# One correction over 1354 columns, and the narrow factor on GpSimd, in a graph-attention loop

## The chip, the cores and the metric

The kernel runs on one core of one Trainium2 chip. A core has a matrix engine (TensorE, PE in the profile, with its weight loads as PEld), VectorE (DVE), ScalarE (ACT), GpSimd (POOL) and a queue engine that issues transfers (SyncE, SP). The engines run side by side, each through its own list of instructions in order, and wait for each other on semaphores. The metric is device time in microseconds of one execution. Half a percent of it is 5.3 us.

## The reference, cut to what matters

Four graph layers run one after the other on x (2708 nodes by 128 features) with the same adjacency matrix adj (2708 by 2708, float32), each followed by a residual sum and a normalization of the rows. The change lies in the second layer, the attention:

```python
XW = X @ W
s_col = XW @ a[0, :f];  s_row = XW @ a[0, f:]
Z1  = leaky_relu(s_row[:, None] + s_col[None, :], negative_slope=0.01)
den = exp(Z1)
num = A @ den
att = where(num != 0, den / where(num != 0, num, 1.0), 0.0)
H   = A @ (att @ XW)
```

The quotient needs 1/num for a matrix of 2708 by 2708. The kernel finds it as exp(-log(num)) on ScalarE, improves it by one Newton step on VectorE, and multiplies it by the part of den that is a maximum of a row value and a column value.

## The kernel before

Earlier stages compute the first layer, the features XW in sorted order (`xws`), the row factors `gb` (a value for each node along the columns, the same on all partitions), the column factors `g_inv`, and the weights `lw` of a short form of A @ den: with the columns sorted, den of a block of columns can be built from the rows of adj that belong to that block and two carried rows of sums.

The layer then runs as a loop of 44 passes, `for i, (h, q) in enumerate(steps)`: two halves h of the output columns (1354 each, `HALF`), and 22 pairs q of blocks in each half. The instructions of the loop stand on every engine in the order in which they are written here, since the loop is under `tc.manual_schedule`. The 1354 columns of a pass are handled in two pieces: wide (1024 columns, `WIDE`) and narrow (330, `NARROW`), because the sums stay in PSUM, where the wide piece has two buffers and the narrow one has one.

One pass, by the names that the change and the prediction use:

- `load(i + 2)`: GpSimd issues two indirect gathers of 126 rows of adj into a strip of `ring` (L1306), and SP issues two small copies of the carried rows into the same strip (L1312). There are three strips, so the strip of pair i + 2 is free when the num of pair i - 1 has been computed. In the first eight passes `fetch_xw` adds one more gather on GpSimd (L895).
- `find_num(i, "narrow")` and `find_num(i + 1, "wide")`: TensorE multiplies the gathered rows by `lw` into `num` (L1428).
- `add(i - 1)`: TensorE multiplies the finished quotient `inv` of the pass before by `xws` and adds it to `hacc` (L1285).
- `find_inv(i, "narrow")`, `find_inv(i + 1, "wide")`: ScalarE computes log and exp (L1260, L1263). In the first half it also scales a tile of `xws` (L1475).
- `mix_1` (L1270): VectorE computes err = inv x num, for each piece. `keep` (L1443) has SP copy two rows of err to `carry`.
- `mix_2` (L1274), the correction: inv = (err - 2) x inv, for each piece.
- `mix_3` (L1277), the factor: inv = max(gb, g_inv) x inv, for each piece.

So TensorE's order is narrow num of pass i, wide num of pass i + 1, hacc of pass i - 1. GpSimd's order is the gathers of pair i + 2, then, in the first passes, the fetch of a tile of `xws`. One more GpSimd instruction, the power of 22 values for `dinv` (L257), belongs to a later layer and stands among the first passes.

Of the kernel before, what the change touches and what calls it, by code (L numbers as in the profile page):

```python
# [8 lines left out]
F32 = mybir.dt.float32  # L9
# [7 lines left out]
P = 128  # L17
# [3 lines left out]
BJ = 62  # L21
# [31 lines left out]
def kernel(  # L53
# [16 lines left out]
    nc = tc.nc  # L70
# [67 lines left out]
    ones = const.tile([P, 1], F32, tag="ones", name="ones")  # L138
    nc.vector.memset(ones, 1.0)

    def load_const(src, cols, name):
        t = const.tile([P, cols], F32, tag=name, name=name)
        nc.sync.dma_start(t, src)
        return t

    def load_rows(src, cols, name):

        return load_const(bass.AP(tensor=src.tensor, offset=src.offset, ap=[[0, P], [1, cols]]), cols, name)

    def row_tile(name):  # L150
        return big.tile([P, T * D], F32, tag="hT", name=name)
# [216 lines left out]
    with tc.tile_pool(name="knn", bufs=1) as knn:  # L368
# [97 lines left out]
        with (  # L466
# [5 lines left out]
            for c in range(C):  # L472
                w = cw[c]
                load_x(chunk_tiles[c])
                parts = [load_panel(g, c, load if g < G - 1 else None) for g in range(G)]
                nc.sync.dma_start(
                    res[:, : FULL - S, cols[c]],
                    adjT[S * P : FULL * P, cols[c]].rearrange("(t p) k -> p t k", p=P),
                )
                if LAST:  # L480
                    nc.sync.dma_start(res[few(c), FULL - S, cols[c]], adjT[FULL * P :, cols[c]])
                both = degp.tile([P, 2, CW], F32, tag="both", name="both")
                nc.vector.tensor_add(both[:, :, :w], parts[0][:, :2, :w], parts[0][:, 2:, :w])
                more = [part[:, n : n + 2, :w] for part in parts[1:] for n in (0, 2)]
                more += [res[:, n : n + 2, cols[c]] for n in range(0, RES, 2)]
                for m in more:
                    nc.vector.tensor_add(both[:, :, :w], both[:, :, :w], m)  # L487
                nc.vector.tensor_add(both[:, 0, :w], both[:, 0, :w], both[:, 1, :w])

                for g in range(min(c, G)):  # L490
                    add_group(c, g, parts[g])
                    if wait is not None:
                        add_group(*wait)
                        wait = None
                if c == C - 1:
# [12 lines left out]
                inv_sqrt(dinv[:, t0:t1], deg[:, t0:t1])  # L508
                scale_rows(y, xs, dinv, ts)
                if c == C - 1:  # L510
                    spread(y[:, FULL, :])
                wait = (c, c, parts[c] if c < G else None, c == C - 1)
                if c == C - 2:
                    w1_sb = load_const(w1, D, "w1")
                    w2_sb = load_const(w2, D, "w2")
                    wa_sb = load_const(w_att, D, "w_att")
                    wl_sb = load_const(w_lap_t, D, "w_lap")
                    wx_sb = load_const(w_cat_t[:D, :], D, "w_cat_x")
                    wh_sb = load_const(w_cat_t[D:, :], D, "w_cat_h")
                    b1_sb = load_rows(b1, D, "b1")  # L520
                    b2_sb = load_rows(b2, D, "b2")
                    bl_sb = load_rows(b_lap, D, "b_lap")
                    bc_sb = load_rows(b_cat, D, "b_cat")
                    a_sb = load_rows(a_att, 2 * D, "a_att")


            def rest(c, g, end=False):
# [726 lines left out]
    del slots[SLOTS:]  # L1254
    more.close()

    def invert(w, num, pool, bufs, sums=True):
        inv = pool.tile([P, w], F32, tag=f"inv{w}", name="inv", bufs=bufs)
        if sums:
            nc.scalar.activation(inv, num[:, :w], AF.Ln, scale=plain[:, 0:1], bias=plain[:, 1:2])  # L1260
        else:
            nc.scalar.activation(inv, num[:, :w], AF.Ln)
        nc.scalar.activation(inv, inv, AF.Exp, scale=-1.0)  # L1263
        return inv

    def mix_1(w, num, inv, pool):
        err = pool.tile([P, w], F32, tag=f"err{w}", name="err")
        nc.vector.tensor_mul(err, inv, num[:, :w])  # L1270
        return err

    def mix_2(inv, err):
        nc.vector.scalar_tensor_tensor(inv, err, 2.0, inv, op0=ALU.subtract, op1=ALU.mult)  # L1274
# [47 lines left out]
    def dense_layer():  # L1322
# [3 lines left out]
        with (  # L1326
# [68 lines left out]
            for h in range(2):  # L1395
                hacc = dps.tile([P, 3 * CW], F32, tag="hacc", name="hacc")
                for q in range(NQ):
# [10 lines left out]
                    inv = invert(HALF, num, dense, 1, sums=False)  # L1408
                    mix_2(inv, mix_1(HALF, num, inv, dense))
                    mix_3(HALF, q, inv, h * HALF)  # L1410
                    add_up(HALF, q, inv, hacc)
                nc.scalar.copy(mT[:, h * HALF : (h + 1) * HALF], hacc[:, :HALF])
    def block_layer():
        with (
# [7 lines left out]
            def find_num(i, piece):  # L1422
                q, (c0, w, bufs) = steps[i][1], pieces[piece]
                num = nums[i, piece] = ops.tile([P, w], F32, tag=f"num{w}", name="num", bufs=bufs)
                for o in range(0, w, CW):
                    e = min(w, o + CW)
                    for n in range(2):
# [2 lines left out]
                            rhs=rows[i][:, n, c0 + o : c0 + e], start=True, stop=True,  # L1430
                        )

            def find_inv(i, piece):
                invs[i, piece] = invert(pieces[piece][1], nums[i, piece], own, 3)

            def keep(i, piece, err):

                (h, q), (c0, w, _) = steps[i], pieces[piece]
                for n in range(2):
                    b = block(2 * q + n) + 1  # L1440
                    if b % CH:
                        o = h * HALF + c0
                        nc.sync.dma_start(  # L1443
                            carry[2 * b : 2 * b + 2, o : o + w], err[n * (BJ + 2) : n * (BJ + 2) + 2, :]
                        )

            def add(i):
# [1 line left out]
                if q == 0:  # L1449
                    haccs[h] = ops.tile([P, 3 * CW], F32, tag="hacc", name="hacc")  # L1450
                for piece, (c0, w, _) in pieces.items():
                    add_up(w, q, invs[i, piece], haccs[h][:, c0 : c0 + w])

            engines = {nc.tensor, nc.vector, nc.scalar, nc.sync, nc.gpsimd}
            with tc.manual_schedule(engines={e.engine for e in engines}):
# [5 lines left out]
                for i, (h, q) in enumerate(steps):  # L1461
# [13 lines left out]
                        nc.scalar.mul(xws[:, q, :], xws[:, q, :], g_col[:, q : q + 1])  # L1475
                    if (h, q) == (1, 0):
                        nc.scalar.copy(mT[:, :HALF], haccs[0][:, :HALF])
                    if i + 1 < len(steps):
                        errs = {}
                        for piece, (c0, w, _) in pieces.items():  # L1480
                            errs[piece] = mix_1(w, nums[i, piece], invs[i, piece], own)
                            keep(i, piece, errs[piece])
                        for piece in pieces:
                            mix_2(invs[i, piece], errs[piece])
                        for piece, (c0, w, _) in pieces.items():
                            mix_3(w, q, invs[i, piece], h * HALF + c0)
                    else:
                        for piece, (c0, w, _) in pieces.items():
                            mix_2(invs[i, piece], mix_1(w, nums[i, piece], invs[i, piece], own))
                            mix_3(w, q, invs[i, piece], h * HALF + c0)  # L1490

                for t0 in range(0, EARLY, WIDE // P):
                    ts = range(t0, min(t0 + WIDE // P, EARLY))
# [130 lines left out]
```

## Time and profile before

| what | us |
|---|---|
| median of 3 runs (1063.95 to 1068.74) | 1066.62 |
| the profiled execution | 1068.2 |
| its span, first to last instruction | 1066.5 |
| TensorE matmul busy in the span | 990.4 |
| VectorE busy | 643.2 |
| ScalarE busy | 339.1 |
| GpSimd busy | 265.6 |
| 88 gathers into ring, mean of one | 1.115 |
| err, 88 instructions of two shapes, mean | 0.853 |
| correction, 88 of two shapes, mean | 0.863 |
| factor, 88 of two shapes, mean | 0.913 |

The span is the time from the first to the last instruction of the program; the execution's own time is 1.7 us longer. Busy times are of one profiled execution. The end of a matmul is modelled in the profile, so where a pace is wanted it is read from the starts of instructions and not from busy time. The three means of VectorE mix a form of 1024 columns with one of 330; in the loop the two forms of err take 1209 and 497 ns, of the correction 1237 and 491, of the factor 1273 and 551 (520 to 700 us of the span).

### The profile page before, as it was taken

The numbers are of one execution on the slowest core, as the hardware profiler recorded it, in microseconds if no ns is written. First come the engines' busy times: TensorE is split into PE (matmuls) and PEld (weight loads), VectorE is DVE, ScalarE is ACT, GpSimd is POOL, SyncE is SP. The second block draws the span as 40 slices with busy tenths as digits, with TensorE's granted clock in tenths as the row PEclk, the third lists the DMA queues.
The fourth block names the chain that finished last, engine by engine and source line by source line (L and its number), as shares of the span: only waits on it lengthen the run. The fifth ranks groups of instructions, "written<-read, shape, count | busy, mean of one in ns | idle before, by whom it ended". The sixth has DMA issues, their size and how long they took to land.

```text
span 1066.5 us, 11423 instructions
## 1 busy us (share of the span) xinstructions
PE 990.4 (93%) x3678; PEld 479.8 (45%) x3678; DVE 643.2 (60%) x1351; ACT 339.1 (32%) x614; POOL 265.6 (25%) x332
## 2 busy tenths in 40 slices
PE   0898999999998999699899999999999999999996
PEld 0345554444434566444333333334444544564444
DVE  5985438999954678764789999995121111132222
ACT  0000125555510235603767777663010100010000
POOL 4000000000447664107774444440121100000000
PEclk9989999999999999699999999999999999999998
DMA  9999350000056756399655546456765856575652
GB/s 338 367 342 249 115 166 1 0 1 1 22 199 211 239 175 207 126 341 306 165 160 131 147 135 164 137 151 208 226 198 173 291 196 202 159 256 170 225 173 67
DMA packets 109363, 190.30 MB, mean 178 GB/s; under 512 B 13650, under 2 KB 46690, under 8 KB 109294
## 3 DMA queue, kind: packets, MB, share of 16 engines
q1 hardware_dynamic: 91582, 151.86, 43.8%
q0 software_dynamic: 17712, 37.62, 12.7%
q8 instruction: 31, 0.51, 0.2%
q14 instruction: 38, 0.31, 0.1%
HBM read 214.37 MB, written 4.16 MB: 205 GB/s over the span
## 4 chain that ended last, share of the span: by engine, by line
PE 80%; DMA 7%; DVE 6%; issue 2%; POOL 2%; ACT 2%; SPq 1%; POOLq 0%; DVEq 0%; ACTq 0%
PE acc L204 34%; PE acc L647 9%; PE hacc L1285 9%; PE num L1428 9%; PE acc L432 7%; DMA res<-in_adjT 3%; PE acc L637 3%; PE acc L1181 2%; DMA got<-y_rows,where 1%; PE mis L289 1%; DMA part<-in_adjT 1%; DVE mask L784 1%; DVE both L487 1%; POOL ring L125 1%; PE mis L1192 1%
## 5 line engine op out<-in xcount | busy, mean ns | idle before, releaser
L1306 POOL DMA_INDIRECT ring<-in_adjT,slot_i x88 | 98.1, 1115 | 101.0 <-PE num L1428 84.8
L1428 PE MATMUL num<-ring,lw 128*64 128x512 f32 (+1 forms) x528 | 113.6, 551 | 3.6 <-DVE err L1270 1.8
L1285 PE MATMUL hacc<-inv,xws 128*128 128x512 f32 (+1 forms) x264 | 111.7, 559 | 0.5 <-ACT inv L1263 0.3
L647 PE MATMUL acc<-zT,z 128*128 128x512 f32 (+4 forms) x264 | 108.5, 558 | 0.0
L1260 ACT ACTIVATE inv<-num,plain 128x1024 f32<-128x1024 f32 x88 | 80.6, 916 | 59.3 <-PE num L1428 58.1
L257 POOL TENSOR_TENSOR rstd<-rstd,minus_half 128x4 f32<-128x4 f32 (+1 forms) x19 | 18.2, 957 | 313.3 <-DVE rstd L256 313.3
L648 ACT COPY key<-acc 128x512 f32<-128x512 f32 (+3 forms) x132 | 70.2, 535 | 59.7 <-issue 29.8
L238 ACT COPY gb<-acc 128x512 f32<-128x512 f32 (+2 forms) x18 | 9.6, 535 | 249.4 <-PE acc L204 249.4
L204 PE MATMUL acc<-ring,y 128*128 128x512 f32 (+2 forms) x192 | 81.8, 555 | 1.6 <-DMA ring<-in_adjT 1.1
L1270 DVE TENSOR_TENSOR err<-inv,num 128x1024 f32<-128x1024 f32 x88 | 74.4, 853 | 13.3 <-ACT inv L1263 12.5
L1285 PEld LDWEIGHTS hacc<-inv,xws 128*128 128x128 f32 x264 | 46.5, 189 | 77.5 <-issue 37.6
L677 POOL DMA_INDIRECT got<-y_rows,where x66 | 70.1, 1063 | 32.8 <-DMA y_rows<-y 9.3
L1277 DVE SCALAR_TENSOR_TENSOR inv<-gb,g_inv,inv 128x1024 f32<-128x1024 f32 x88 | 77.0, 913 | 0.1
L204 PE MATMUL acc<-ring,xs 128*128 128x512 f32 (+2 forms) x192 | 76.7, 542 | 0.0
L204 PE MATMUL acc<-ring,carry 128*128 128x512 f32 (+2 forms) x192 | 74.5, 542 | 0.0
L204 PE MATMUL acc<-ring,m_rows 128*128 128x512 f32 (+2 forms) x192 | 74.3, 542 | 0.0
L1274 DVE SCALAR_TENSOR_TENSOR inv<-err,inv 128x1024 f32<-128x1024 f32 x88 | 72.6, 863 | 0.1
L647 PEld LDWEIGHTS acc<-zT,z 128*128 128x128 f32 (+1 forms) x264 | 47.6, 188 | 54.9 <-issue 49.5
L1263 ACT ACTIVATE inv<-inv 128x1024 f32<-128x1024 f32 x88 | 67.6, 768 | 2.8
L649 DVE MAX8 near<-key 128x8 f32<-128x2708 f32 (+1 forms) x22 | 65.5, 2978 | 4.8 <-ACT key L648 4.8
L574 POOL TENSOR_TENSOR slot_e<-near,sim 128x44 f32<-128x44 f32 (+2 forms) x3 | 0.7, 244 | 271.5 <-DVE d2inv L602 267.3
L650 DVE FIND_INDEX8 where<-near,key 128x8 uint32<-128x2708 f32 (+1 forms) x22 | 65.4, 2972 | 0.0
(327 smaller groups left out, 1340.0 us busy)
## 6 DMA issues: line engine op xcount, KB each, us to landing
ring<-in_adjT SPq DMA_DIRECT2D x86, 1024.0 KB
ring<-in_adjT SPq DMA_DIRECT2D x19, 768.0 KB
part<-in_adjT SPq DMA_DIRECT2D x12, 1024.0 KB
ring<-in_adjT SPq DMA_DIRECT2D x19, 552.0 KB
res<-in_adjT SPq DMA_DIRECT2D x4, 1280.0 KB
more<-in_adjT SPq DMA_DIRECT2D x4, 1024.0 KB
part<-in_adjT SPq DMA_DIRECT2D x3, 768.0 KB
part<-in_adjT SPq DMA_DIRECT2D x3, 552.0 KB
```

Source lines behind the costliest of these rows:

```text
L204: nc.tensor.matmul(accs[c][: lhsT.shape[-1], :w], lhsT=lhsT, rhs=src, start=start, stop=stop)
L432: nc.tensor.matmul(accs[c][:, : cw[c]], lhsT=y[:, i, :], rhs=src[:, : cw[c]], start=first, stop=last)
L647: nc.tensor.matmul(pks[c][:p, : cw[c]], lhsT=z2[:, :p], rhs=zT[:, cs], start=False, stop=True)
L648: nc.scalar.copy(key[:p, cs], pks[c][:p, : cw[c]])
L677: nc.gpsimd.indirect_dma_start(out=got[:p, :], out_offset=None, in_=y2_rows[:, :], in_offset=bass.IndirectOffsetOnAxis(ap=where[:p, t, k : ...
L1260: nc.scalar.activation(inv, num[:, :w], AF.Ln, scale=plain[:, 0:1], bias=plain[:, 1:2])
L1270: nc.vector.tensor_mul(err, inv, num[:, :w])
L1274: nc.vector.scalar_tensor_tensor(inv, err, 2.0, inv, op0=ALU.subtract, op1=ALU.mult)
L1277: nc.vector.scalar_tensor_tensor(inv, gb[:, col : col + w], g_inv[:, q : q + 1], inv, op0=ALU.max, op1=ALU.mult)
L1285: nc.tensor.matmul(haccs[:, o:e], lhsT=xws[:, q, :], rhs=inv[:, o:e], start=(q == 0), stop=(q == NQ - 1))
L1306: nc.gpsimd.indirect_dma_start(out=rows[i][:KC, n, :], out_offset=None, in_=adj_half[:, :], in_offset=bass.IndirectOffsetOnAxis(ap=slot_i[ ...
L1428: nc.tensor.matmul(num[n * (BJ + 2) : (n + 1) * (BJ + 2), o:e], lhsT=lw[:, 2 * q + n, :], rhs=rows[i][:, n, c0 + o : c0 + e], start=True, ...
```

## The change

The two pieces of `inv` become parts of one tile of 1354 columns, with three buffers as before, and those of `err` one tile with two buffers. The loop then issues, in each pass but the last, one correction over all 1354 columns on VectorE instead of two. The factor of the wide piece stays on VectorE. That of the narrow piece moves to GpSimd, in two instructions: a maximum of 330 columns of gb with g_inv into a new tile `early`, and a product of the narrow part of inv with it. In the last pass both pieces are corrected and multiplied on VectorE as before. The tile `early` holds w1, b1 and a_att until then, which had tiles of their own; the same eleven loads of constants are issued. The function `dense_layer`, which is the other arm of a branch and does not run with these inputs, is adapted to the same helpers.

In the built program GpSimd's order becomes: the gathers of pair i + 2, the fetch (first eight passes), the maximum of pass i, the product of pass i. The power for `dinv` moves from between two gathers to the place between the first maximum and the first product. TensorE, ScalarE and SP keep their order.

```diff
-    def invert(w, num, pool, bufs, sums=True):
-        inv = pool.tile([P, w], F32, tag=f"inv{w}", name="inv", bufs=bufs)
+    def invert(inv, num, sums=True):
...
-    def mix_1(w, num, inv, pool):
-        err = pool.tile([P, w], F32, tag=f"err{w}", name="err")
-        nc.vector.tensor_mul(err, inv, num[:, :w])
-        return err
...
+            def part(v, piece):
+                c0, w, _ = pieces[piece]
+                return v[:, c0 : c0 + w]
+
             def find_inv(i, piece):
-                invs[i, piece] = invert(pieces[piece][1], nums[i, piece], own, 3)
+                if i not in invs:
+                    invs[i] = own.tile([P, HALF], F32, tag="inv", name="inv", bufs=3)
+                invert(part(invs[i], piece), nums[i, piece])
...
+                    err = own.tile([P, HALF], F32, tag="err", name="err")
+                    for piece in pieces:
+                        nc.vector.tensor_mul(part(err, piece), part(invs[i], piece), nums[i, piece])
+                        if i + 1 < len(steps):
+                            keep(i, piece, err)
                     if i + 1 < len(steps):
-                        errs = {}
-                        for piece, (c0, w, _) in pieces.items():
-                            errs[piece] = mix_1(w, nums[i, piece], invs[i, piece], own)
-                            keep(i, piece, errs[piece])
-                        for piece in pieces:
-                            mix_2(invs[i, piece], errs[piece])
-                        for piece, (c0, w, _) in pieces.items():
-                            mix_3(w, q, invs[i, piece], h * HALF + c0)
+                        nc.gpsimd.tensor_scalar_max(
+                            early[:, :NARROW], gb[:, h * HALF + WIDE : (h + 1) * HALF], g_inv[:, q : q + 1]
+                        )
+                        mix_2(invs[i], err)
+                        mix_3(WIDE, q, part(invs[i], "wide"), h * HALF)
+                        nc.gpsimd.tensor_mul(part(invs[i], "narrow"), part(invs[i], "narrow"), early[:, :NARROW])
                     else:
                         for piece, (c0, w, _) in pieces.items():
-                            mix_2(invs[i, piece], mix_1(w, nums[i, piece], invs[i, piece], own))
-                            mix_3(w, q, invs[i, piece], h * HALF + c0)
+                            mix_2(part(invs[i], piece), part(err, piece))
+                            mix_3(w, q, part(invs[i], piece), h * HALF + c0)
```

More of the change, by code (lines that the diff above doesn't have):

```diff
@@ L139, with load_const, load_rows @@
     nc.vector.memset(ones, 1.0)
-    def load_const(src, cols, name):
-        t = const.tile([P, cols], F32, tag=name, name=name)
+    def load_const(src, cols, name, t=None):
+        if t is None:
+            t = const.tile([P, cols], F32, tag=name, name=name)
         nc.sync.dma_start(t, src)
         return t
-    def load_rows(src, cols, name):
-        return load_const(bass.AP(tensor=src.tensor, offset=src.offset, ap=[[0, P], [1, cols]]), cols, name)
+    def load_rows(src, cols, name, t=None):
+        return load_const(bass.AP(tensor=src.tensor, offset=src.offset, ap=[[0, P], [1, cols]]), cols, name, t)
+    early = const.tile([P, 4 * D], F32, tag="early", name="early")
     def row_tile(name):
@@ L513 @@
                 if c == C - 2:
-                    w1_sb = load_const(w1, D, "w1")
+                    w1_sb = load_const(w1, D, "w1", early[:, :D])
                     w2_sb = load_const(w2, D, "w2")
@@ L519 @@
                     wh_sb = load_const(w_cat_t[D:, :], D, "w_cat_h")
-                    b1_sb = load_rows(b1, D, "b1")
+                    b1_sb = load_rows(b1, D, "b1", early[:, D : 2 * D])
                     b2_sb = load_rows(b2, D, "b2")
@@ L523 @@
                     bc_sb = load_rows(b_cat, D, "b_cat")
-                    a_sb = load_rows(a_att, 2 * D, "a_att")
+                    a_sb = load_rows(a_att, 2 * D, "a_att", early[:, 2 * D :])
             def rest(c, g, end=False):
@@ L1255 @@
     more.close()
-    def invert(w, num, pool, bufs, sums=True):
-        inv = pool.tile([P, w], F32, tag=f"inv{w}", name="inv", bufs=bufs)
+    def invert(inv, num, sums=True):
         if sums:
-            nc.scalar.activation(inv, num[:, :w], AF.Ln, scale=plain[:, 0:1], bias=plain[:, 1:2])
+            nc.scalar.activation(inv, num, AF.Ln, scale=plain[:, 0:1], bias=plain[:, 1:2])
         else:
-            nc.scalar.activation(inv, num[:, :w], AF.Ln)
+            nc.scalar.activation(inv, num, AF.Ln)
         nc.scalar.activation(inv, inv, AF.Exp, scale=-1.0)
-        return inv
-    def mix_1(w, num, inv, pool):
-        err = pool.tile([P, w], F32, tag=f"err{w}", name="err")
-        nc.vector.tensor_mul(err, inv, num[:, :w])
-        return err
     def mix_2(inv, err):
@@ L1407, in dense_layer @@
                         nc.scalar.mul(xws[:, q, :], xws[:, q, :], g_col[:, q : q + 1])
-                    inv = invert(HALF, num, dense, 1, sums=False)
-                    mix_2(inv, mix_1(HALF, num, inv, dense))
+                    inv = dense.tile([P, HALF], F32, tag="inv", name="inv")
+                    err = dense.tile([P, HALF], F32, tag="err", name="err")
+                    invert(inv, num[:, :HALF], sums=False)
+                    nc.vector.tensor_mul(err, inv, num[:, :HALF])
+                    mix_2(inv, err)
                     mix_3(HALF, q, inv, h * HALF)
@@ L1443, in keep @@
                         nc.sync.dma_start(
-                            carry[2 * b : 2 * b + 2, o : o + w], err[n * (BJ + 2) : n * (BJ + 2) + 2, :]
+                            carry[2 * b : 2 * b + 2, o : o + w], part(err, piece)[n * (BJ + 2) : n * (BJ + 2) + 2, :]
                         )
@@ L1451, in add @@
                 for piece, (c0, w, _) in pieces.items():
-                    add_up(w, q, invs[i, piece], haccs[h][:, c0 : c0 + w])
+                    add_up(w, q, part(invs[i], piece), haccs[h][:, c0 : c0 + w])
             engines = {nc.tensor, nc.vector, nc.scalar, nc.sync, nc.gpsimd}
```

## The prediction

> **What bounds the kernel now.** The page first: which engine is full, and what the chain that ended last is made of.
>
> ```profile
> PE 990.4 (93%) x3678; PEld 479.8 (45%) x3678; DVE 643.2 (60%) x1351; ACT 339.1 (32%) x614; POOL 265.6 (25%) x332
> PE 80%; DMA 7%; DVE 6%; issue 2%; POOL 2%; ACT 2%; SPq 1%; POOLq 0%; DVEq 0%; ACTq 0%
> ```
>
> TensorE carries 80% of the chain over the whole span. Only the block loop (508.6 to 731 us) is edited, so the second view is the table by stage, for the settled part of that loop (columns: us; busy PE, PEld, DVE, ACT, POOL; PE clock; DMA share; GB/s).
>
> ```profile
> 559.70:711.50 151.80, 151.80 (x562) 56.83 (x560) 149.88 (x186) 109.42 (x138) 65.59 (x62) 1.00 0.53 143
> ```
>
> PE is busy all the time, but VectorE too, to 99%, so the table doesn't say which of them sets the pace. The timeline of one pass does (start, duration, engine).
>
> ```profile
> 603.15 2.50 PE L1428 MATMUL num<-ring,lw 128*64 128x330 f32 x12
> 603.94 1.73 DVE L1270 TENSOR_TENSOR err<-inv,num 128x1024 f32<-128x1024 f32 x2
> 604.00 0.63 ACT L1260 ACTIVATE inv<-num,plain 128x330 f32<-128x330 f32 x1 [0.59 <-PE num L1428]
> 604.22 1.05 POOL L1306 DMA_INDIRECT ring<-in_adjT,slot_i  x1 [2.48 <-PE num L1428]
> 604.66 0.48 ACT L1263 ACTIVATE inv<-inv 128x330 f32<-128x330 f32 x1
> 605.58 1.06 POOL L1306 DMA_INDIRECT ring<-in_adjT,slot_i  x1 [0.30 <-issue]
> 605.58 2.54 PE L1285 MATMUL hacc<-inv,xws 128*128 128x512 f32 x6
> 605.59 1.66 DVE L1274 SCALAR_TENSOR_TENSOR inv<-err,inv 128x1024 f32<-128x1024 f32 x2
> 607.17 1.74 DVE L1277 SCALAR_TENSOR_TENSOR inv<-gb,g_inv,inv 128x1024 f32<-128x1024 f32 x2
> 608.05 2.50 PE L1428 MATMUL num<-ring,lw 128*64 128x330 f32 x12
> ```
>
> A pass is 4.90 us (603.15 to 608.05). The factor of the pass before (L1277, the pair begun at 602.27) is over near 604.0, and hacc, which reads it, starts at 605.58: PE is not waiting for VectorE, it is 1.5 us behind it. VectorE's own back-to-back pace, seen while it was catching up (L1270 at 532.06 and at 536.82), is 4.76. So PE sets 4.90 and VectorE is held to it by num and ACT's inverse.
>
> The third resource is GpSimd, with one job here: as soon as the narrow num matmuls free a strip (604.0), it issues the two gathers of three passes later.
>
> ```profile
> POOL ring L1306 <- PE num L1428: 80.5, 33, 3.5
> DMA to landing us min/median/max: 3.6/4.4/5.5
> ```
>
> The waits say that POOL stands idle in front of these gathers, waiting for PE; the second line (the view of L1306, 560 to 720 us) is their time to land. The second gather of each pair lands last: its single rows give 4.4 to 5.5, mean 4.9. Call X the time from the start of pass i's narrow num to the landing of pair i+3. Now X = 1.07 (604.22 - 603.15) + 1.36 (second issue) + 4.9 = 7.33. The rows are wanted by the wide num in pass i+2, 0.61 into it: 2 x 4.90 + 0.61 = 10.41. The cover is **3.08 us**.
>
> **What the Trainium skill says.** "GPSIMD Engine Reference", section 3.1 Elementwise, puts a two-input fp32 add of 2048 columns at 4497 ns on GpSimd, about twice VectorE. The trace is milder: 128 columns 474 ns mean (L1532; 0.45 undisturbed), 384 in 827, 2176 in 3817. "SBUF — State Buffer", section Who interferes with whom: a VectorE instruction with two SBUF inputs contends with a GpSimd instruction that reads SBUF, and the one that starts first holds the shared port for its whole length. The trace agrees where it can be seen:
>
> ```profile
> 302.34 0.83 POOL L606 TENSOR_TENSOR y<-xs,d2inv 128x384 f32<-128x384 f32 x1
> 302.76 0.42 DVE L571 TENSOR_TENSOR near<-near,node 128x8 f32<-128x8 f32 x1 [0.60 <-ACT near L570]
> 531.38 4.03 POOL L257 TENSOR_TENSOR dinv<-dinv,minus_half 128x22 f32<-128x22 f32 x1
> ```
>
> The 8-column add takes 424 ns where this line's shortest takes 148, and ends as POOL's does. The opposite order is weaker: the power of 22 columns starts inside L1277 and takes 0.26 more than 3 and 4 columns (860 and 1013 ns) extrapolate to, while VectorE beside it isn't stretched. The err product (L1270) has one SBUF input (num is in PSUM); L1274 and L1277 have two.
>
> **The change, part by part.**
>
> *VectorE, 43 of 44 passes.* The correction of 1024 and of 330 columns becomes one of 1354: 1.22 + 330 x (1.22 - 0.49)/694 = 1.57 us, against a pitch of 1.55 for the two. The narrow factor (pitch 0.47) goes. Each step now follows directly on the one it needs, which shows 0.03 to 0.05 after the end rather than a 0.08 overlap. Sum: 1.13 + 0.50 + 0.05 + 1.57 + 0.03 + 1.28 - 0.08 = 4.48, from 4.76. Worth nothing: the cover is PE's 4.90.
>
> *GpSimd, new, 43 times:* a max of 330 columns with one tensor input, a form not seen in this trace: 0.19 (one column, L586) + 330 x 0.83 ns (memsets of 128 and 2816 columns, 205 and 2448 ns) = 0.46 at the least, 0.75 if it is as dear as the product; I take 0.46. And a product of 330 with two: 0.45 + 202 x (827 - 450)/256 = 0.75 (the page's price, as an estimate: 330 x 2.2 = 0.73). POOL has 2.48 us idle in a pass, so the amount fits. The place doesn't.
>
> *The queue.* In the built order POOL now has: gathers of i+2, (fetch of xws), max i, product i, gathers of i+3. The product waits for the correction of pass i, and the gathers that used to start at 1.07 are behind it. From the start of pass i's narrow num:
> - 2.02: narrow err starts (603.15 to 605.17, ACT's 0.63 + 0.48 before it), as now
> - 2.57: correction starts (0.50 + 0.05); 4.14: it ends (1.57)
> - then the wide factor and POOL's product both want the port. VectorE follows itself after 0.03; POOL follows VectorE after 0.08 to 0.145 in its rstd rows (L256 to L257). So the factor gets it, and the product waits to 5.45 (1.28)
> - 6.22: product done (0.02 + 0.75); 6.44: first gather (0.22 after a tensor instruction, as at 535.63); 7.80: second; **12.70: landed**.
>
> The max follows the previous gathers, near 3.3 of its pass, inside the two-input correction; held to 4.14 it goes first, pushing factor and product back by up to 0.46: X = 13.16. It won't collide in every pass, the more so while fetches stand before it; I take 12.95.
>
> X is over 10.41 by 2.5, so num waits for the gather. From wide num to the next narrow num PE needs 4.29 (4.90 - 0.61); pair i+3 thus starts 4.29 + X after pair i, a pitch of (4.29 + 12.95)/3 = **5.75 us**. The sort of wait is there already: while fetches and the power stood in this queue, passes began at 540.77, 546.97, 553.23 and 559.09, 6.2, 6.3 and 5.9 apart, with PE waiting for the gather.
>
> *Start.* The power (4.03) now stands between max 0 and product 0; working the rows above through, wide num of pair 4 starts near 530.5 (now 526.7). From there to pair 43 are 13 links of 17.24: 754.6, now 721.25. **Sum: +33 us.**
>
> *Free:* one tile for w1, b1 and a_att is the same eleven DMAs with its readers done 200 us earlier; one err tile makes the wide err wait also for the narrow carry copies of two passes before (issued some 5 us earlier); SP's carry copies keep their order, ahead of the gathers. hacc's last third waits for the product (6.7) and runs after 8. Later layers hold the same order on every engine.
>
> **Against the times.** Span 1066.5 + 33 = 1099.5; the profiled execution is 1068.2 (1.7 outside the span), the median of runs 1066.6: 1066.6 + 33 = 1099.6.
>
> **Rivals.**
> - *Late gathers without the port conflict* (the product runs beside the factor): X = 4.14 + 0.10 + 0.75 + 0.22 + 1.36 + 4.9 = 11.47, pitch 5.25, pair 4 near 529: 529 + 13 x 15.76 = 733.9, +12.6: 1079. For it: L257 stretched nothing beside it. Against: L571. Chance 0.22.
> - *The cover holds:* no port conflict (11.47) and gathers that land in 3.6 instead of 4.9 give X = 10.17, under 10.41, and since PE already sets the pace nothing is won: 1067. Against: all second gathers seen took 4.4 or more. Chance 0.06.
> - *PE's gaps are VectorE's.* Bare spacing of a pass's matmuls is 2 x (4 x 0.43 + 2 x 0.275) = 4.54; 0.36 is lost at the two changes between num and hacc. Were these waits on VectorE, a shorter chain would give 0.36 x 33 settled passes = 12: 1055. It decides only if X stays under 2 x 4.54 + 0.61 = 9.7, and hacc's 1.5 us of slack speaks against it. Chance 0.03.
> - *A further blocking,* max and product each behind a VectorE instruction in every pass: X 13.7, +43: 1110. Chance 0.03.
>
> **The numbers.** Forecast 0.66, own range 1092 to 1109. The range of 8 in 10 takes in the rival at 1079 with its spread of gather times (4.4 to 5.5), and the upper bounds of max and product: 1074 to 1112. A difference of 0.5% (5.3 us) is what can be told from none: faster 0.03, same 0.06, slower 0.91.
>
> **What would show it.** L1306 released by the product or nothing but its queue, not by num; PE waits for ring gathers, tens of us in all; pass pitch 5.6 to 5.9, VectorE under 90% busy in the loop; the product's row near 2 us if its record includes the hold at the port, else 0.75 and begun when the wide factor ends. Wrong if the pitch stays 4.9, or if PE waits for the product (hacc) or VectorE instead of DMA.

## The result, and the profile after

The changed kernel takes 1125.88 us (median of 6 runs, 1121.63 to 1128.63) against 1069.01 for the kernel before beside it: ratio **1.0532, interval 1.0507 to 1.0558**. The loss is 57 us where the prediction had 33, outside its range. The profiled execution is 1128.63 us, its span 1126.8. In it the loop takes 56.4 us longer than before, some 18 of them in its first ten passes.

The page, the lines that answer to those shown of before: engine totals, the chain by engine, and the two groups that stand against each other.

```profile
PE 1029.8 (91%) x3678; PEld 489.3 (43%) x3678; DVE 633.3 (56%) x1265; ACT 338.8 (30%) x614; POOL 397.6 (35%) x418
PE 67%; DMA 12%; POOL 7%; issue 5%; DVE 5%; ACT 2%; SPq 0%; POOLq 0%; ACTq 0%; DVEq 0%
L1425 PE MATMUL num<-ring,lw 128*64 128x512 f32 (+1 forms) x528 | 149.2, 562 | 24.3 <-DMA ring<-in_adjT,slot_i 21.7
L1300 POOL DMA_INDIRECT ring<-in_adjT,slot_i x88 | 126.9, 1442 | 23.4 <-issue 16.5
```

TensorE has lost 13% of the chain; DMA, GpSimd and "issue" have it. The gathers (L1300, formerly L1306) are issued for 1442 ns each where they took 1115, though nothing about them was edited.

The table by stage over 215 us of the settled loop (columns as before: us; busy PE, PEld, DVE, ACT, POOL; PE clock; DMA share; GB/s):

```profile
560.00:775.00 215.00, 201.59 (x628) 71.13 (x628) 160.86 (x141) 123.27 (x156) 190.02 (x143) 1.00 0.45 122
```

VectorE fell to 75% (160.86 of 215) and GpSimd rose from 43% to 88%. What the missing 12% is, the groups on GpSimd in the same window show (count, busy us, mean ns, idle before and its releasers):

```profile
L1300 POOL DMA_INDIRECT ring<-in_adjT,slot_i x70 | 102.0, 1457 | 18.3 <-issue 13.3 <-PE num L1425 3.2 <-DVE inv L1268 1.7
L1487 POOL TENSOR_SCALAR early<-gb,g_inv 128x330 f32<-128x330 f32 x36 | 51.7, 1437 | 1.6
L1492 POOL TENSOR_TENSOR inv<-inv,early 128x330 f32<-128x330 f32 x35 | 35.3, 1008 | 4.8 <-DVE inv L1268 2.1
L898 POOL DMA_INDIRECT xws<-xw_rows,row_j x2 | 2.1, 1028 | 0.6 <-issue 0.6
```

Busy and idle make up the whole window. Of the 25.3 us idle, only 1.7 + 2.1 end with the correction (L1268) and 3.2 with num (L1425); the rest is the small gap that GpSimd leaves between two of its instructions. **GpSimd is full**, and its product has waited for the correction in 2 of 35 passes only. Two gathers, a maximum, a product and four gaps are 2 x 1.457 + 1.437 + 1.008 + 0.70 = 6.06 us; the pass, from narrow num to narrow num, takes 6.07 (mean from pass 10 on, 4.89 to 7.25), 4.90 before.

Why the gathers became dear is in the timeline of one pass (start, duration, engine; GpSimd, VectorE's correction and factor, and the wide num that waits):

```profile
612.07 1.11 POOL L1300 DMA_INDIRECT ring<-in_adjT,slot_i  x1 [0.18 <-issue]
613.26 1.57 DVE L1268 SCALAR_TENSOR_TENSOR inv<-err,inv 128x1354 f32<-128x1354 f32 x1
613.49 2.29 POOL L1300 DMA_INDIRECT ring<-in_adjT,slot_i  x1 [0.30 <-PE num L1425]
614.87 1.29 DVE L1271 SCALAR_TENSOR_TENSOR inv<-gb,g_inv,inv 128x1024 f32<-128x1024 f32 x1
615.82 1.31 POOL L1487 TENSOR_SCALAR early<-gb,g_inv 128x330 f32<-128x330 f32 x1
617.21 0.88 POOL L1492 TENSOR_TENSOR inv<-inv,early 128x330 f32<-128x330 f32 x1
618.27 1.11 POOL L1300 DMA_INDIRECT ring<-in_adjT,slot_i  x1 [0.18 <-issue]
618.51 1.94 PE L1425 MATMUL num<-ring,lw 128*64 128x512 f32 x6 [0.34 <-DMA ring<-in_adjT,slot_i]
```

GpSimd goes round without a pause: 1.11 + 0.30 + 2.29 + 0.04 + 1.31 + 0.08 + 0.88 + 0.19 = 6.20. The second gather starts 0.23 into the correction and ends 0.94 after its end: it looks as if its issue had begun only then. The maximum starts inside the factor and ends 0.97 after it. The correction was over at 614.83, but the product begins at 617.21, because two held instructions, the gather and the maximum, stand before it in the queue. The times of all gathers (min, median, max) and TensorE's waits for them, same window, two views:

```profile
L1300 POOL DMA_INDIRECT ring<-in_adjT,slot_i x70: 1065/1112/2459, 562.3 to 772.8; - x70
DMA to landing us min/median/max: 3.4/3.9/4.8
```

```profile
PEld num L1425 <- DMA ring<-in_adjT,slot_i: 39.5, 34, 2.3
PE num L1425 <- DMA ring<-in_adjT,slot_i: 13.5, 22, 1.7
POOL ring L1300 <- PE num L1425: 3.2, 12, 0.3
```

Most gathers issue in 1.1 us as ever, some take up to 2.46. The landings in that view are of first gathers alone, none of them held (before, the view had both of a pair). For the second gather the start of the first matmul that reads it tells more: from pass 10 to 39 TensorE waits there in 26 of 30 passes, until 5.20 us after the start of a held gather on average and 5.06 after that of one that isn't held. So a held gather lands hardly later, counted from its start; what it delays is the queue behind it. The last wait was 80.5 us before, and was GpSimd's spare time.

### The profile page after: what moved, and what is told of

The parts are those of the page before. It is cut to its first block, busy times and chain, and to the rows that moved or that the text cites. A ratio compares the mean times of both kernels' runs of the same rounds, so it can differ in the third digit from the quotient of the medians.

```text
span 1126.8 us, 11472 instructions
## 1 busy us (share of the span) xinstructions
PE 1029.8 (91%) x3678; PEld 489.3 (43%) x3678; DVE 633.3 (56%) x1265; ACT 338.8 (30%) x614; POOL 397.6 (35%) x418
## 3 DMA queue, kind: packets, MB, share of 16 engines
q0 software_dynamic: 17712, 37.62, 12.1%
## 4 chain that ended last, share of the span: by engine, by line
PE 67%; DMA 12%; POOL 7%; issue 5%; DVE 5%; ACT 2%; SPq 0%; POOLq 0%; ACTq 0%; DVEq 0%
PE acc L207 32%; PE acc L650 9%; DMA ring<-in_adjT,slot_i 8%; PE acc L435 7%; PE num L1425 5%; POOL ring L1300 3%; PE hacc L1279 3%; DMA res<-in_adjT 3%; PE acc L640 2%; PE acc L1184 2%; POOL early L1487 1%; PE mis L292 1%; DMA part<-in_adjT 1%; DVE mask L787 1%; DVE both L490 1%
## 5 line engine op out<-in xcount | busy, mean ns | idle before, releaser
L1425 PE MATMUL num<-ring,lw 128*64 128x512 f32 (+1 forms) x528 | 149.2, 562 | 24.3 <-DMA ring<-in_adjT,slot_i 21.7
L1300 POOL DMA_INDIRECT ring<-in_adjT,slot_i x88 | 126.9, 1442 | 23.4 <-issue 16.5
L1483 DVE TENSOR_TENSOR err<-inv,num 128x1024 f32<-128x1024 f32 x88 | 75.3, 859 | 73.7 <-ACT inv L1265 72.7
L1262 ACT ACTIVATE inv<-num,plain 128x1024 f32<-128x1024 f32 x88 | 80.5, 914 | 115.9 <-PE num L1425 109.0
L1425 PEld LDWEIGHTS num<-ring,lw 128*64 128x64 f32 x528 | 43.2, 136 | 112.3 <-DMA ring<-in_adjT,slot_i 55.7
L1268 DVE SCALAR_TENSOR_TENSOR inv<-err,inv 128x1354 f32<-128x1354 f32 (+2 forms) x45 | 70.2, 1561 | 4.3
```

The lines of the kernel that those rows point to most:

```text
L1262: nc.scalar.activation(inv, num, AF.Ln, scale=plain[:, 0:1], bias=plain[:, 1:2])
L1300: nc.gpsimd.indirect_dma_start(out=rows[i][:KC, n, :], out_offset=None, in_=adj_half[:, :], in_offset=bass.IndirectOffsetOnAxis(ap=slot_i[ ...
L1425: nc.tensor.matmul(num[n * (BJ + 2) : (n + 1) * (BJ + 2), o:e], lhsT=lw[:, 2 * q + n, :], rhs=rows[i][:, n, c0 + o : c0 + e], start=True, ...
L1483: nc.vector.tensor_mul(part(err, piece), part(invs[i], piece), nums[i, piece])
```

## The experiments

The question was how much of the loss is the **place** of the gathers (behind a product that waits for the correction), and how much is the **amount** of work on GpSimd, with the holds that instructions suffer beside VectorE. The runs were spread over several chips, on which the kernel before took 1069 us or 1097 to 1102, so every kernel is given as a ratio to the kernel before on its own chip. The pace is from the starts of narrow num: the sum of the first ten passes, and the mean from pass 10 on.

| kernel | ratio, interval | first ten, us | later pass, us |
|---|---|---|---|
| before | 1 | 53.7 | 4.90 |
| after | 1.0532, 1.0507 to 1.0558 | 71.4 | 6.07 |
| merge_only | 1.0006, 0.9990 to 1.0023 | 54.0 | 4.90 |
| two_corrections | 1.0470, 1.0432 to 1.0509 | 66.7 | 6.04 |
| wait_alone | 1.0346, 1.0307 to 1.0386 | 64.2 | 5.69 |
| work_alone | 1.0552, 1.0517 to 1.0587 | 67.5 | 6.14 |
| gathers_first | 1.0633, 1.0589 to 1.0677 | 72.7 | 6.24 |
| one_input | 1.0224, 1.0187 to 1.0262 | 61.8 | 5.38 |
| no_max | 1.0400, 1.0344 to 1.0457 | 61.0 | 5.90 |
| first_no_max | 1.0083, 1.0056 to 1.0109 | 60.9 | 4.90 |
| first_one_input | 1.0075, 1.0050 to 1.0100 | 59.0 | 4.91 |
| before_late_fetch | 0.9998, 0.9972 to 1.0024 | 50.1 | 5.02 |
| late_fetch_last_power | 0.9948, 0.9923 to 0.9972 | 50.6 | 4.90 |

### The two halves of the change

**merge_only**: the one correction stays, and VectorE does the factor over all columns.

```diff
-                        nc.gpsimd.tensor_scalar_max(early[:, :NARROW], ...)
                         mix_2(invs[i], err)
-                        mix_3(WIDE, q, part(invs[i], "wide"), h * HALF)
-                        nc.gpsimd.tensor_mul(part(invs[i], "narrow"), part(invs[i], "narrow"), early[:, :NARROW])
+                        mix_3(HALF, q, invs[i], h * HALF)
```

> The one correction of 1354 columns stays, and VectorE does the factor over all 1354 columns; GpSimd has its gathers alone. Both theories: GpSimd and the gathers are as before, so the kernel is within 3 us of before (1069), VectorE's chain staying under PE's 4.9 us. If merging itself costs (each VectorE step now waits for the one before), the pitch rises over 4.9 and it is 5 us or more slower.

**two_corrections**: GpSimd has the narrow factor, and the two corrections of before are kept.

```diff
-                        mix_2(invs[i], err)
+                        for piece in pieces:
+                            mix_2(part(invs[i], piece), part(err, piece))
```

> The other half of the change alone: GpSimd has the maximum and the product as in the changed kernel, but VectorE makes the correction in two instructions, of 1024 and of 330 columns, as before. SUM, PLACE and HOLD: GpSimd's work, place and holds are the same but for the places at which a held instruction can get in (after 1.2 us instead of 1.57), so it is 45 to 62 us over before, within 8 us of the changed kernel. If the merging carries part of the loss, it is 15 us or more faster than the changed kernel.

The merge alone changes nothing that can be measured (VectorE stays busy for 117.85 of 120 us in its settled loop), and the move alone costs 4.7%: the loss is the move of the narrow factor to GpSimd.

### The wait, the work, and the order

**wait_alone**: GpSimd keeps its two instructions, their wait and their place, for 8 columns only; VectorE does 1346.

```diff
+            FEW = 8
-                            early[:, :NARROW], gb[:, h * HALF + WIDE : (h + 1) * HALF], g_inv[:, q : q + 1]
+                            early[:, :FEW], gb[:, (h + 1) * HALF - FEW : (h + 1) * HALF], g_inv[:, q : q + 1]
-                        mix_3(WIDE, q, part(invs[i], "wide"), h * HALF)
-                        nc.gpsimd.tensor_mul(part(invs[i], "narrow"), part(invs[i], "narrow"), early[:, :NARROW])
+                        mix_3(HALF - FEW, q, invs[i][:, : HALF - FEW], h * HALF)
+                        nc.gpsimd.tensor_mul(invs[i][:, HALF - FEW :], invs[i][:, HALF - FEW :], early[:, :FEW])
```

> The split between VectorE and GpSimd is moved from 1024 + 330 columns to 1346 + 8: GpSimd still makes a maximum and a product that waits for the correction, in the same places of its queue, but of 8 columns (about 0.2 us each, as the small GpSimd instructions of the trace). Theory PLACE: correction ends at 4.2, product waits for the factor of 1346 columns (1.6 us) and ends near 6.0, second gather at 7.5, landed at 12.4 or later: pitch 5.6 or more, 25 to 45 us over before. Theory SUM: GpSimd's sum is at most 1.11 + 0.3 + 2.3 + 0.2 + 0.2 + 0.4 = 4.5, under PE's 4.9, so within 8 us of before.

A pass takes 5.69. One of its products in the timeline, with the factor beside it:

```profile
645.40 1.62 DVE L1271 SCALAR_TENSOR_TENSOR inv<-gb,g_inv,inv 128x1346 f32<-128x1346 f32 x1
645.63 1.46 POOL L1493 TENSOR_TENSOR inv<-inv,early 128x8 f32<-128x8 f32 x1
```

Eight columns take 1.46 us and end 0.07 after the factor: this is the hold at the port that the prediction gave the product, with nearly no work in it. The gathers are at their bare 1.093 here, since GpSimd is early enough to issue them outside the two-input instructions. So the place, together with the hold of the product, costs two thirds of the loss even when the work is next to none. The hold is somewhat longer here than in the changed kernel, since VectorE's factor has 1346 columns and not 1024.

**work_alone**: VectorE does all 1354 columns; GpSimd does a maximum and a product of 330 into `early` that nobody waits for.

```diff
+                        nc.gpsimd.tensor_mul(
+                            early[:, :NARROW], early[:, :NARROW], gb[:, h * HALF + WIDE : (h + 1) * HALF]
+                        )
                         mix_2(invs[i], err)
-                        mix_3(WIDE, q, part(invs[i], "wide"), h * HALF)
-                        nc.gpsimd.tensor_mul(part(invs[i], "narrow"), part(invs[i], "narrow"), early[:, :NARROW])
+                        mix_3(HALF, q, invs[i], h * HALF)
```

> VectorE does the factor over all 1354 columns, and GpSimd still makes the maximum and a product of 330 columns in the same places, but the product multiplies the maximum by gb into the scratch tile and waits for nothing that VectorE makes; its result is not used. Theory PLACE: nothing waits for the correction, gathers start when the strip is free, pitch 4.9 to 5.0, within 8 us of before. Theory SUM: GpSimd has the same instructions, 1.11 + 0.3 + 1.06 to 2.3 + 1.12 to 1.31 + 0.88 + 0.3 = 4.8 to 6.2 a pass, and the pitch follows that sum: 20 to 55 us over before if the holds stay.

No GpSimd instruction waits for the correction, and the pass takes 6.14: gather 1.477, maximum 1.643, product 0.899, with the gaps 6.16. The amount, with the holds that it meets, is also enough for the whole loss. The two causes don't add: each is a limit, and the later one sets the pass.

**gathers_first**: maximum and product of pass i - 1 are issued in pass i, behind the gathers of i + 2. This takes the place away and leaves the amount.

```diff
+            def finish(i):
+                h, q = steps[i]
+                nc.gpsimd.tensor_scalar_max(
+                    early[:, :NARROW], gb[:, h * HALF + WIDE : (h + 1) * HALF], g_inv[:, q : q + 1]
+                )
+                nc.gpsimd.tensor_mul(part(invs[i], "narrow"), part(invs[i], "narrow"), early[:, :NARROW])
...
                         fetch_xw(xws, late_q.pop(0))
+                    if i:
+                        finish(i - 1)
```

> The maximum and the product of pass i-1 are issued on GpSimd in pass i, behind the gathers of pair i+2 and not in front of them; all work is the same. Theory PLACE (the gathers start late because they stand behind a product that waits for the correction): the gathers start again when the strip is free (1.07 us into the pass), land in time, the pitch of a pass goes back to 4.9 us and the kernel to within 8 us of before. Theory SUM (GpSimd's own instructions, with the time that two-input VectorE instructions hold them, fill the pass: 1.11 + 0.30 + 2.3 + 0.04 + 1.31 + 0.08 + 0.88 + 0.18 = 6.2 us): the order changes nothing in the sum but the holds, the pitch stays between 5.3 and 6.2 and the kernel 20 to 55 us over before.

The pass takes 6.24, more than after. The longest wait of TensorE for another engine in the loop, over the whole run, and the GpSimd groups from 600 to 740 us:

```profile
PEld hacc L1279 <- POOL inv L1455: 66.6, 29, 3.9
```

```profile
L1300 POOL DMA_INDIRECT ring<-in_adjT,slot_i x46 | 64.5, 1403 | 11.2 <-issue 6.0 <-PE num L1425 2.6 <-PE hacc L1279 1.5
L1452 POOL TENSOR_SCALAR early<-gb,g_inv 128x330 f32<-128x330 f32 x23 | 35.3, 1534 | 1.0
L1455 POOL TENSOR_TENSOR inv<-inv,early 128x330 f32<-128x330 f32 x22 | 27.5, 1252 | 1.8
```

GpSimd is as full as before (64.5 + 35.3 + 27.5 + gaps of 14.0 = 141.3 of 140 us), only now TensorE's hacc waits for the late product instead of num for the late gather. The theory that the place alone was to blame fell here.

### The hold, and both causes at once

**one_input**: VectorE's correction (in two pieces again, which two_corrections shows to matter little) and factor take `num` (in PSUM) as their second operand in place of the SBUF one; everything on GpSimd is as after. The layer's quotient is left out; VectorE's instructions take as long as before (1214 and 492 ns, 1274 for the wide factor).

```diff
-                        mix_2(invs[i], err)
-                        mix_3(WIDE, q, part(invs[i], "wide"), h * HALF)
+                        for piece in pieces:
+                            nc.vector.scalar_tensor_tensor(
+                                part(invs[i], piece), part(err, piece), 2.0, nums[i, piece], op0=ALU.subtract, op1=ALU.mult
+                            )
+                        nc.vector.scalar_tensor_tensor(
+                            part(invs[i], "wide"), part(invs[i], "wide"), g_inv[:, q : q + 1], nums[i, "wide"],
+                            op0=ALU.max, op1=ALU.mult,
+                        )
```

> The order and the GpSimd instructions of the changed kernel, but every VectorE instruction of the loop has one operand in SBUF and one in PSUM: the correction multiplies by num instead of inv (in the two pieces of num), and the factor multiplies by num instead of taking gb, so the quotient is left out. Theory HOLD (two-input VectorE instructions hold GpSimd's instructions that start under them): gathers go back to 1.06 to 1.11 us, the maximum to 1.12, the product to 0.88 in every pass; GpSimd's sum is 2.2 + 1.12 + 0.88 + 0.69 of gaps = 4.9, and what is left is the late landing, 4.2 + 0.1 + 0.9 + 0.2 + 1.4 + 4.9 = 11.7 us into the pass, pitch (4.29 + 11.7)/3 = 5.3: 10 to 22 us over before. Without HOLD (the instructions are simply that long while VectorE runs): durations and pitch stay as in the changed kernel, 6.0 to 6.3, 50 us or more over before.

```profile
L1300 POOL DMA_INDIRECT ring<-in_adjT,slot_i x53 | 57.8, 1090 | 14.4 <-issue 10.5 <-PE num L1425 2.3 <-PE hacc L1279 1.6
L1487 POOL TENSOR_SCALAR early<-gb,g_inv 128x330 f32<-128x330 f32 x26 | 29.2, 1121 | 1.1
L1498 POOL TENSOR_TENSOR inv<-inv,early 128x330 f32<-128x330 f32 x26 | 23.1, 890 | 15.2 <-DVE inv L1491 15.1
```

(GpSimd's groups from 600 to 740 us.) With one SBUF operand on VectorE not one GpSimd instruction is stretched: from pass 10 on, gathers take 1.065 to 1.115 us, the maximum 1.104 to 1.130, the product 0.884 to 0.897. Of the maxima 22 of 33 and of the products 32 of 33 start under a correction or a factor, so for these two the hold is shown, and the bare times are given. For gathers this run shows nothing, as only 1 of 63 starts there (23 of 63 in the changed kernel); first_one_input below has more. GpSimd now has slack (15.1 us of waiting for the correction), and the pass of 5.38 is the place alone: the second gather starts 6.71 after narrow num, 4.9 to land makes X = 11.61, and (4.29 + 11.61)/3 = 5.30. Over passes 10 to 39, from which these are means, the pass is 5.30 as well.

**no_max**: the maximum is made in the first pass only and left out in the others, which use it again.

```diff
+                        if i == 0:
-                        nc.gpsimd.tensor_scalar_max(
+                            nc.gpsimd.tensor_scalar_max(
```

> The maximum is made in the first pass alone and used for all (left out: the maximum of the other passes for the narrow columns); the product and the order of the changed kernel stay. Theory SUM alone: GpSimd has 1.3 to 1.5 less, about 4.7 with gaps, so the pitch is 4.9 to 5.0, within 8 us of before. Theory PLACE alone: the product still ends behind correction and wide factor, second gather at 7.8, landed at 12.7: pitch 5.6 to 5.8, 28 to 40 us over before. Both at work: 5.2 to 5.7.

GpSimd isn't full (26.3 us of waiting for the correction from 600 to 740), yet the pass takes 5.90, over the 5.2 to 5.7 that were expected with both at work. The product (1.493 mean) and the second gather are still held, and the landing sets the pass. Taking off one instruction doesn't help while the place stays.

**first_no_max** and **first_one_input**: the order of gathers_first, with the maximum left out, or with VectorE's operands as in one_input. (The same edits as above.)

> Gathers in front of the product as in e1, and the maximum made in the first pass alone as in e6. If the sum and the place are together the whole cause, nothing is left: GpSimd's sum is 2.12 + 0.88 to 1.3 + 0.6 = 3.6 to 4.0 and the gathers start at 1.07 into the pass: pitch 4.9, within 6 us of before. If anything else is at work (VectorE held by GpSimd, hacc waiting for the product), 10 us or more are left.

> Gathers in front as in e1 with all of GpSimd's work, and VectorE with one SBUF operand as in e5 (quotient left out as there). HOLD with SUM and PLACE: no instruction is held and no gather stands behind the product; the sum of 4.8 to 4.9 is as long as PE's pass, so pitch 4.9 to 5.1 and 0 to 12 us over before. If e1's loss had another cause than the holds, it stays at 50 us or more over before.

The groups of first_one_input, 560 to 725 us, and below them the gathers of first_no_max, 600 to 740:

```profile
L1300 POOL DMA_INDIRECT ring<-in_adjT,slot_i x66 | 72.0, 1090 | 18.5 <-PE num L1425 8.1 <-issue 8.0 <-PE hacc L1279 1.2
L1452 POOL TENSOR_SCALAR early<-gb,g_inv 128x330 f32<-128x330 f32 x35 | 39.2, 1119 | 1.6
L1455 POOL TENSOR_TENSOR inv<-inv,early 128x330 f32<-128x330 f32 x35 | 31.1, 890 | 3.4 <-DVE inv L1497 0.6
```

```profile
L1300 POOL DMA_INDIRECT ring<-in_adjT,slot_i x50 | 79.2, 1585 | 13.2 <-issue 13.2
```

Both are back at 4.90 and 4.91. In first_one_input 40 of the 62 gathers from pass 10 on start under a correction or a factor, and none takes more than 1.117: that shows the hold on gathers. In first_no_max gathers are still held (1585 ns on average) and the settled pass loses nothing, since the round with them still fits into the pass. So a hold costs only where the queue has no room for it. The settled loop's loss is gone when the place and either the holds or the maximum are gone, and with the order alone (6.24), the hold alone (5.38) or the maximum alone (5.90) taken away it isn't.

Most of the 0.8% left are the first ten passes, 5 to 7 us longer than before, where fetches still share the queue. In first_one_input passes 3 to 7, with a fetch in each, take 6.12 to 6.14: GpSimd's bare round of 4.78 (summed below) and 1.33 for a fetch with its gap are 6.11.

### The first passes of the kernel before

These passes lose time in the kernel before as well (passes 6 to 8 take 6.20, 6.25 and 5.87). **before_late_fetch** starts the fetches four passes later, in passes 4 to 11, and moves the power to pass 15.

```diff
-                    if late_q:
+                    if late_q and i >= 4:
...
+                    if i == 15:
+                        inv_sqrt_of(dinv, deg, DEG_EPS, power=True)
...
-        inv_sqrt_of(dinv, deg, DEG_EPS)
+        if first == 0:
+            inv_sqrt_of(dinv, deg, DEG_EPS)
```

> The kernel before, with the eight fetches of xws issued in passes 4 to 11 instead of 0 to 7, and the power of 22 values in pass 15 instead of among passes 0 to 4. In the kernel before, passes that began at 540.8, 547.0, 553.2 took 6.2, 6.3 and 5.9 us where the settled ones take 4.9, with fetches, the power and held gathers in GpSimd's queue. If the queue is the cause, these 3.5 us go and the kernel is 2 to 5 us faster than before; the four or five fetches of later passes fit into GpSimd's 2.4 idle us a pass. If the start of the loop waits for something else (the carried rows, the DMA of the panels), it is within 1 us of before.

The first ten passes take 50.1 instead of 53.7, as expected, but the kernel isn't the 2 to 5 us faster that were expected, since the power gives it back in its new place: it waits for VectorE, then occupies the queue, and the gather behind it starts 4.1 us after it. One later pass takes 7.78.

```profile
610.63 3.89 POOL L257 TENSOR_TENSOR dinv<-dinv,minus_half 128x22 f32<-128x22 f32 x1 [3.18 <-DVE dinv L256]
614.74 1.47 POOL L1306 DMA_INDIRECT ring<-in_adjT,slot_i  x1 [0.22 <-PE num L1428]
```

**late_fetch_last_power** puts the power in pass 42, behind all gathers.

```diff
-                    if i == 15:
+                    if i == 42:
```

> The kernel before, with the eight fetches of xws in passes 4 to 11 instead of 0 to 7 as in the run before, but the power for dinv in pass 42, where no gather into ring is left behind it in the queue. The reading is that a fetch or a power delays PE only when it stands ahead of a gather whose cover (3.08 us) it eats up together with other fetches. Then passes 6 to 9 take 4.89 instead of 6.20, 6.25, 5.87 as in the run before, and the stall of 7.8 at the power's new place doesn't come back: ratio 0.996 to 0.998 (3 to 4 us faster). The rival, that the time lost at the start of the loop comes back anyway because the later layer waits for dinv or the fetched tiles, gives 0.999 to 1.003.

The stall is gone: from the first narrow num to the last 212.4 us (215.4 in the profile of before), and the ratio is 0.9948, interval 0.9923 to 0.9972. The loop's 3.0 us is 0.3%; what the rest of 0.5% would be, if it is real, isn't located. By its ratio this kernel is the fastest of all, by half a percent.

## Why the prediction was wrong in size, by its own steps

**What held.** Slower, with TensorE waiting for gathers that stand behind the product: the waits show it (53.0 us for `ring`; for num GpSimd waits 3.2 us in all). The merge is worth nothing (merge_only). VectorE's pass was to be 4.48 us and is 160.86 x 6.07/215 = 4.54. The hold of the product is real (wait_alone). The start was right: wide num of pair 4 at 531.41, forecast 530.5. From there on the loop left the forecast: wide num of pair 43 came at 777.08 and not 754.6, 22.5 us late. That is nearly all of the 24 us by which the medians miss. It came in two parts: pair 10 was 10.4 late already, and from there to pair 43 another 12.1 were lost, 0.37 in each pass.

**The step that failed** is "POOL has 2.48 us idle in a pass, so the amount fits. The place doesn't." The amount, with what it meets on the way, doesn't fit: GpSimd's round is 6.06 us and sets the pass of 6.07. The forecast's 5.75 follows another path, in which the product waits for the correction and the factor; in the changed kernel it waited for the correction twice in 35 passes. That 5.75 lies so near 6.07 is in part chance. Term by term, means of passes 10 to 39 from the start of narrow num:

| term | forecast | measured |
|---|---|---|
| maximum, bare | 0.46 (0.75 at most) | 1.12 |
| product, bare | 0.75 | 0.88 |
| product done | 6.22, 6.68 with the maximum | 7.17 |
| second gather starts | 7.80, up to 8.26 | 8.76 |
| its issue takes | 1.06 | 1.88 |
| X, at the first matmul that reads this gather | 12.95 | 13.90 |
| pitch (measured from pass 10 to the last) | 5.75 | 6.07 |

Of the 0.95 us that X was short, the later start is 0.71 (against 8.05 as taken) and the landing 0.24.

The maximum was priced from memsets, which read no tensor; it costs more than twice as much and more than the product. The Trainium skill, "GPSIMD Engine Reference", section 4.1 Engine selection, calls one-input operations there roughly line-rate against VectorE, and two-input ones about two times slower: here the one-input maximum (1.12 us for 330 columns) is the slower of the two. And with bare times alone a round of GpSimd is 1.11 + 0.30 + 1.07 + 0.04 + 1.12 + 0.08 + 0.88 + 0.18 = 4.78 of 4.90: it fits by a tenth of a microsecond. With a hold of more than that it doesn't.

The other miss of this size is the **gather's issue**, taken as 1.06 wherever it falls; held, the second gather pushes maximum, product and the next gathers back by 0.82 on average. The Trainium skill, "SBUF — State Buffer", section Who interferes with whom, says that a VectorE instruction with two SBUF inputs contends with a GpSimd instruction that reads SBUF. The prediction applied it to maximum and product and not to the gather. That a gather counts was in the trace of before, in its first passes (timeline):

```profile
520.87 1.75 DVE L1277 SCALAR_TENSOR_TENSOR inv<-gb,g_inv,inv 128x1024 f32<-128x1024 f32 x2
521.05 2.03 POOL L1306 DMA_INDIRECT ring<-in_adjT,slot_i  x1 [0.91 <-PE num L1428]
...
524.08 1.63 DVE L1274 SCALAR_TENSOR_TENSOR inv<-err,inv 128x1024 f32<-128x1024 f32 x2
524.75 1.87 POOL L895 DMA_INDIRECT xws<-xw_rows,row_j  x1 [0.30 <-issue]
```

The first row merges a 1024 and a 330 column factor, the first of them over near 522.15: the gather ends 0.93 after that. In the settled loop of before the gathers miss the hold by a narrow chance of timing (60 of 62 take 1.05 or 1.06): one starts at 605.58 and the correction at 605.59. Once the product moves them, that is over. With bare times and no place problem the pass is 4.91, with the place alone 5.38, with place and holds 6.07: of the 1.17 us lost per pass 0.48 is the place, and 0.69 comes with the holds. Counted in the other order the shares differ, since the holds without the place (gathers_first) cost 1.34.

**A term set at nothing** is the fetches after pair 4. "From there to pair 43 are 13 links of 17.24" takes passes 4 to 7 as settled ones, but each still has a fetch in GpSimd's queue, 1.33 us with its gap. Four of them are 5.3 us, and six passes of 0.37 are 2.2: by this estimate 7.5 of the 9.5 us that were lost from pair 4 to pair 10. No run moves the fetches in the changed kernel.

**A slip that cost little.** The prediction has the rows of a second gather wanted at the start of the wide num, 0.61 into its pass. The first matmul that reads them starts 0.43 later, so the cover before was 3.5 us and not 3.08, and what TensorE has left after it 3.86 and not 4.29. With these the forecast's own X would have given a pitch of 5.60. In the changed kernel TensorE needed 4.30 there, with other waits in it, so that the forecast's 4.29 came out right by luck.

**The rivals.** "Late gathers without the port conflict" is what one_input makes: worked out at a pitch of 5.25, measured 5.38, with a ratio of 1.0224 where 1079 would be 1.012; 8 of its 24 us are in the first ten passes. "The cover holds" and "PE's gaps are VectorE's" are out: the first because the pitch didn't stay at 4.90, the second by first_no_max, where VectorE is busy for 110 of 120 us (119 before) and TensorE keeps its 4.90. "A further blocking" was nearest in kind and had 0.03, with the maximum and the product blocked and not the gathers. **A sign** that was wrong: the product's row near 2 us. In after it comes so late that the factor is mostly over (1.01 mean); the long rows are the gather's and the maximum's.

After the last narrow num the changed kernel's profile is another 4 us longer (344.9 against 340.8), which no experiment addressed. The profiles of the other kernels have 341.0 to 344.5 there, so it need not belong to the change; the granted clock was 0.95 in the last 126 us, and 0.97 in the last 122 before.

## What to carry to other kernels

Before work is moved to an engine that issues transfers, add up a whole round of its queue with gaps, and ask of each instruction in it, the issuing ones too, what it meets at its new time of day: a free instruction may be free only where it now falls. Look for that in the rows that already fall elsewhere, such as the first passes of a loop. And where two limits lie close together, taking one away shows only part of it, or nothing (here 6.07 to 5.38, 5.90 or even 6.24); only the pair taken away together shows that both were the cause.

## What the runs showed of the hardware

- The issue of an indirect gather is held by a VectorE instruction with two SBUF inputs under which it starts: up to 2.46 us for 1.07 to 1.11 bare, ending some 0.94 after that instruction. With one of the inputs in PSUM it never was from pass 10 on (1.065 to 1.117 in first_one_input). What of the issue is held, such as its reading of the row numbers (`slot_i`), no run shows.
- A held issue lands hardly later, counted from its start: where TensorE waited for the rows of a second gather, it read them 5.20 us after the start of a held one and 5.06 after that of one not held (21 and 5 gathers of the changed kernel; 5.17 in one_input, where none is held). What pays is the queue behind it.
- The waiting GpSimd instruction can get in between two VectorE instructions that follow each other directly (not always: the fetch of 524.75 above began under the first of two corrections, over at 525.30, and ended 0.90 after the second), and the second of these is stretched for part of its time only: a maximum that started at 602.21 under a correction ended at 604.46, 0.97 after it, and the factor begun at 603.53 took 1.44 for 1.28. The Trainium skill, "SBUF — State Buffer", section SBUF: two separate sides, says that the one that starts first has the port for its whole length; that fits the held side, and not this stretch of VectorE, which is 0.16 where the maximum ran on for 0.93.
- On GpSimd a maximum of 330 columns with one tensor input and a value for each partition (1.12 us) costs more than the product of two tensors (0.88).
